# First layer and first head: probabilities turned by 32x32 blocks and transfers, and a program order held in a table

## Chip, cores and metric

The kernel runs on one core of one Trainium2 chip. The metric is the device time in microseconds (us) of one execution, given as the median of several; less is better. Five engines work side by side: TensorE (in the profile PE, its weight loads PEld), VectorE (DVE), ScalarE (ACT), GpSimd (POOL) and SyncE (SP), which here only issues transfers. Each takes its own instructions in program order, so an instruction that waits holds up everything behind it on its engine.

## What is computed

Two blocks in float32, over 2 sequences of 1024 tokens and 256 channels. The first is causal attention with one head of width 256, the second causal attention with 16 heads of width 128 and rotary positions, followed by a mixture of four experts. The reference, cut:

```python
x_norm = (x - mu) / sqrt(var + EPS) * gamma + beta          # first layer
q, k, v = x_norm @ qkv[:, :256], x_norm @ qkv[:, 256:512], x_norm @ qkv[:, 512:]
attn = softmax(where(causal, q @ k.T / sqrt(256), -inf))
x = layernorm(x + (attn @ v @ o_proj + x))
...
h = layernorm(x, ln1_w, ln1_b)                              # second layer
q, k, v = h @ wq + bq, h @ wk + bk, h @ wv + bv             # 16 heads of 128
q, k = rotary(q), rotary(k)
probs = softmax(where(causal, q @ k.T / sqrt(128), min))
h = x + (concat(probs @ v) @ wo + bo)
m = top2_of_4_experts(layernorm(h, ln2_w, ln2_b))
out = layernorm(x + (h + m))
```

## The kernel before

**Rows and steps.** Attention is cut into rows, one for each block of 128 queries. `RowA(b, i)` is row i (0 to 7) of sequence b in the first layer, `RowB(u, i)` the same of a unit u, that is one head of one sequence in the second layer. There are 16 RowA and 32 units of 8 RowB, in all 272 steps; step t starts the scores of row t. A0 = 16 is the step of the first RowB, and unit 0 is steps 16 to 23. `step(t, fillers)` writes out the instructions of a step: scores of row t, fillers registered for that step by `at`, `first`, `mid`, `end_of` and `late`, then the normalisation, transposition and output of rows that started one to ten steps earlier. The program order of all engines comes from this loop, and after the last step from a list written by hand (`all_of`, `hidden`, `m_bias`, `m_residual`, `o_stats`, `o_finish`: experts and the last normalisation).

**A row.** TensorE makes the scores in PSUM (L365, L780). `softmax_row` lets VectorE cut the diagonal block by a mask (L324) and take the maximum (L326), and ScalarE the exponential with its sum (L331). The probabilities then lie with queries on the partitions. The product with the values needs them the other way round, with keys on the partitions. There are two ways to turn them:

- `transposed_row` (L343): TensorE transposes each 128x128 block against the identity into PSUM; ScalarE copies the first four blocks of a row to SBUF (L348), VectorE the others (L346). All RowA, all of unit 0 and the first four rows of the last unit go this way. Of a RowA the turned tile `pTa` is the stationary operand of the product (L387), and the division by the row's sum comes with the residual (L395). In unit 0 VectorE divides first (L796).
- By blocks (units 1 to 31, apart from those four rows): ScalarE divides (L794), VectorE transposes each 32x32 block in place in the row (L811, `STREAM_TRANSPOSE`), and after four rows `gather` issues sixteen transfers on SP's queue (L833) that put the blocks where the whole transposition has them. The tile is then the moving operand of the product (L854), mostly eight to ten steps after the scores, as the table PARTS says. `blocks_sb` are two SBUF areas for the block form: `pair_sb`, and the tile `x1` of the first layer's output, which goes to DRAM first (`x1_out`) and comes back for the end (`x1_back`).

**Work beside the rows.** `b_project` and `seven_products` make queries, keys and values (seven products in place of eight, on sums that GpSimd and VectorE form); GpSimd turns queries and keys by their positions, four instructions for each half of a head (`rotated`, L477 to L479), which wait in a list and are written out at the end of a step. `a_residual` scales a tile of `x1` on ScalarE (L438), and GpSimd adds the output bias into the residual tile `h` (L441). `output_sums`/`seven_outputs` project a head pair onto `h`. Weights of later groups are loaded on SP's queue.

Of the kernel before, what the change touches and what calls it, by code (L numbers as in the profile page):

```python
# [18 lines left out]
P = 128  # L19
# [4 lines left out]
TABLE = "natural_log_exp_and_others"  # L24


@with_exitstack
def kernel(
# [62 lines left out]
    bank = [0]  # L91

    def acc_tile(k=None):

        bank[0] = 1 - bank[0] if k is None else k
        return ps_acc.tile([P, 512], F32, tag=f"acc{bank[0]}", name="pa")
# [25 lines left out]
    pair_sb = const.tile([P, 2 * 4 * D], F32, name="pair_sb")  # L122
    x1_dram = dpool.tile([P, NTT, D], F32, name="x1_dram")
    xr = x.rearrange("b (n p) d -> p (b n) d", p=P)
    a_ctx = ExitStack()
    apool = a_ctx.enter_context(tc.tile_pool(name="apool", bufs=1))
# [84 lines left out]
    def transposed(dst, xn, c, wcol, bcol):  # L211
# [13 lines left out]
    va = [apool.tile([P, NT, D], F32, tag=f"va{b}", name="va") for b in range(B)]  # L225
    wT = va[1].rearrange("p i d -> p (i d)")[:, : 3 * DC * D].rearrange(
        "p (w c n) -> p w c n", w=3, c=DC
    )
# [121 lines left out]
    pTa = work.tile([P, 2, NT, P], F32, tag="pT0", name="pTa", bufs=1)  # L350

    class RowA:


# [3 lines left out]
        def scores(self):  # L358
# [13 lines left out]
            self.pr, self.sm, _ = softmax_row(sc, i)  # L372

        def normalise(self):
            self.rs = small.tile([P, 1], F32, tag="rsa", name="rsa")
            nc.vector.reciprocal(self.rs, self.sm)

        def transpose(self):
            pT = pTa[:, self.i % 2]
            transposed_row(self.pr, self.i, lambda c0, n: pT[:, c0 : c0 + n, :])  # L380
            self.pT = pT

        def output(self):
            b, i = self.b, self.i
            pa = acc_tile()
            for c in range(i + 1):
                nc.tensor.matmul(  # L387
                    pa[:, :D],
                    lhsT=self.pT[:, c, :],
# [44 lines left out]
    def a_residual(b, i):  # L434
# [6 lines left out]
        nc.gpsimd.tensor_tensor(h[:, b * NT + i, :], t, bo_sb, ALU.add)  # L441
# [28 lines left out]
    def rotated(t, cs, eng=nc.gpsimd):  # L470

        def rest():
            rot = bpool.tile([P, 512], F32, tag="rot", name="rot")
# [51 lines left out]
    def weight_sums(name):  # L525
        t = lpool.tile([P, 3, HD], F32, tag=f"S{name}", name="S")
# [15 lines left out]
    def seven_products(g, b, name, wide):  # L542
# [35 lines left out]
        def kept(pa, i):  # L578
            t = lpool.tile([P, 512], F32, tag="part", name="part", bufs=2)
            moved(t, pa, i)  # L580
            return t
# [16 lines left out]
        def p1():  # L598
# [3 lines left out]
            st["k"] = bank[0]  # L602
# [28 lines left out]
        def p7():  # L631
# [3 lines left out]
            bank[0] = st["k"]  # L635

        if wide:
            return [p1, p2, p4, p3, p6, p5, p7]
        return [p1, p2, p3, p4, p5, p6, p7]
# [53 lines left out]
    def seven_outputs(g, b):  # L693
        st = {}

        def piece(bank_, w, x, start, i, k):
            def run():
                if start:
                    if bank_ == "a":
                        st["a"] = acc_tile()  # L700
                        st["k"] = bank[0]
# [18 lines left out]
                bank[0] = st["k"]  # L720

            return run
# [24 lines left out]
    blocks_sb = pair_sb, x1.rearrange("p n d -> p (n d)")  # L747
    NU = B * H
    U0, U1, GP = 1, (NU - 1, NU), 2
# [3 lines left out]
        1: {8: range(0, 2), 9: range(2, 4), 10: range(4, 8)},  # L753
        (NU - 2, 1): {8: range(0, 4), 9: range(4, 8)},
# [5 lines left out]
    class RowB:  # L760
# [12 lines left out]
        def scores(self):  # L773
# [13 lines left out]
            self.pr, self.sm, self.exponential = softmax_row(sc, i, self.blocks)  # L787
# [10 lines left out]
        def pT_tile(self, j):  # L798
            shape = [P, 4 * (j + 1), 512]
            if self.u == units[-1] and j == 0:  # L800
                return bpool.tile(shape, F32, tag="vg", name="pT")
            return work.tile(shape, F32, tag=f"pT{j}", name="pT", bufs=1)

        def transpose(self):
            i, j = self.i, self.i // 4
            if self.blocks:


                n = 4 * (i + 1)
                z = blocks_sb[j].rearrange("p (m i s) -> p i m s", i=4, s=32)  # L810
                nc.vector.transpose(  # L811
                    z[:, i % 4, :n, :], self.pr[:, : n * 32].rearrange("p (m s) -> p m s", s=32)
                )
# [8 lines left out]
        def gather(self, part):  # L822

            i, j = self.i, self.i // 4
            n = 4 * (j + 1)
            if part == 0:
                pTs[self.u, j] = self.pT_tile(j)
            pT = pTs[self.u, j]
            z = blocks_sb[j].rearrange("p (c b x) -> p b c x", b=4, x=P)
            for d in range(part * 4 // GP, (part + 1) * 4 // GP):  # L830
                for b in range(4):
                    a = (b + d) % 4
                    nc.sync.dma_start(pT[ts(b, 32), :, ts(a, P)], z[ts(a, 32), b, :n])  # L833

        def output(self, lag):
# [5 lines left out]
            if (g, b) not in aT:  # L841
                aT[g, b] = bpool.tile([P, GH, S], F32, tag="aT", name="aT")
# [32 lines left out]
    steps = [(RowA(b, i), []) for b in range(B) for i in range(NT)]  # L875
# [7 lines left out]
    steps += [(RowB(u, i), []) for u in units for i in range(NT)]  # L883

    firsts, mids, ends, lates = {}, {}, {}, {}

    def at(step, f, *args):
        steps[step][1].append(lambda: f(*args))

    def first(step, f, *args):  # L890
        firsts.setdefault(step, []).append(lambda: f(*args))

    def mid(step, f, *args):
        mids.setdefault(step, []).append(lambda: f(*args))

    def end_of(step, f, *args):
        ends.setdefault(step, []).append(lambda: f(*args))
# [9 lines left out]
    def late(step, f, *args):  # L907
        lates.setdefault(step, []).append(lambda: f(*args))


    XS0 = (14, 14, 15, A0 + 3)
    XS1 = (A0 + 8, A0 + 9, A0 + 10, A0 + 11)
# [5 lines left out]
    weights_transposed(0)  # L918
    a_stats(0, J0)
    weights_transposed(1)  # L920
    a_norm(0, 0)
    a_stats(0, J1)
    weights_transposed(2)
    weight_product(wqk, 0, lambda kc: wT[:, 1, kc, :], SCALE_A)
    parameters(0)
    for c in range(DC):
        a_transposed(0, 0, c)
    a_norm(0, 1)
    weight_product(wvo, 2, lambda kc: op_sb[:, kc, :], 1.0)
    a_query(0, 0, 0)  # L930
    a_query(0, 0, 1)
    a_transposed(0, 1, 0)
# [560 lines left out]
```

## Time and profile before

| | |
|---|---|
| median of 3 runs | 1172.46 us (1172.44 to 1173.12) |
| the profiled execution | 1174.3 us, of which the span from the first to the last instruction is 1172.5 us |
| mean granted TensorE clock | 0.996 |
| busy: TensorE | 1144.5 us (98%) |
| busy: VectorE | 846.2 us (72%) |
| busy: ScalarE | 641.5 us (55%) |
| busy: GpSimd | 808.3 us (69%) |

Busy time is a sum over the span; the stages differ. From 0 to about 110 us the first layer runs, from there to about 1040 us the heads, and after that the experts. A row of the groups' view reads: source line, engine, operation, output and inputs, shape, count, then busy time in us and mean ns of one, then idle time of the engine just ahead of it and who ended it. Matrix products in float32 appear as two instructions each, transpositions as one. Matmuls overlap, so the mean duration of one is longer than its distance to the next; the distance is what it costs in a full stream.

### The profile page before, as it was taken

The page shows a single profiled execution, that of the slowest core. Times are in us where ns is not written, and L with a number is a line of the kernel's source. Part 1 is how long each engine was busy: PE and PEld are TensorE (multiplying, and loading weights), DVE is VectorE, ACT ScalarE, POOL GpSimd, SP SyncE. Part 2 cuts the span into 40 slices and gives each one's busy share as a digit, 9 for nine tenths or more (in the row PEclk, how much of TensorE's full clock was granted, in tenths as well). Part 3 has the DMA queues.
Part 4 walks back from the last instruction along what each step waited for, and adds up shares of the span by engine and source line. Part 5 has one row for each costly group of instructions (what it writes and reads, how often), then busy time and mean ns, then how long its engine had stood idle before and what let it go on. Part 6 is the DMA issues. An engine that isn't in the chain of part 4 may idle for free.

```text
span 1172.5 us, 15932 instructions
## 1 busy us (share of the span) xinstructions
PE 1144.5 (98%) x4736; PEld 730.4 (62%) x4736; DVE 846.2 (72%) x1802; ACT 641.5 (55%) x1221; POOL 808.3 (69%) x758
## 2 busy tenths in 40 slices
PE   7999989999999999999999999999999999999997
PEld 5675745475756565666656565757575656656665
DVE  4555686778787868686868687877778788576575
ACT  3334256566566565656565656566656556452344
POOL 4005999988897989698969896989889998003100
PEclk9999999999999999999999999999999999999999
DMA  6000012566555555555555545555555668404011
GB/s 185 0 1 0 28 72 56 128 134 135 132 120 124 118 135 118 117 119 135 117 120 114 133 108 121 139 134 129 134 137 134 147 133 174 107 23 138 1 37 36
DMA packets 222965, 122.36 MB, mean 104 GB/s; under 512 B 17340, under 2 KB 221184, under 8 KB 222368
## 3 DMA queue, kind: packets, MB, share of 16 engines
q1 hardware_dynamic: 217696, 111.35, 40.7%
q0 software_dynamic: 1776, 4.89, 1.6%
q10 hardware_dynamic: 3408, 5.11, 1.2%
q8 instruction: 38, 0.62, 0.2%
q14 instruction: 47, 0.39, 0.1%
HBM read 20.62 MB, written 4.19 MB: 21 GB/s over the span
## 4 chain that ended last, share of the span: by engine, by line
PE 91%; DVE 5%; ACT 1%; DMA 1%; SPq 1%; issue 1%; ACTq 0%; DVEq 0%
PE av L854 20%; PE sc L780 20%; PE pa L562 11%; PE pa L553 5%; PE pa L708 5%; PE pa L1275 5%; PE pe L1298 4%; PE pc L562 4%; PE sc L365 3%; PE pa L387 2%; PE pc L553 2%; PE pc L708 2%; PE pa L660 1%; PE pa L306 1%; PE pa L293 1%; PE pt L343 1%
## 5 line engine op out<-in xcount | busy, mean ns | idle before, releaser
L794 ACT ACTIVATE pr<-pr,rs 128x640 f32<-128x640 f32 (+1 forms) x244 | 190.5, 781 | 219.2 <-DVE rs L792 219.0
L780 PE MATMUL sc<-Twk,Twq 128*128 128x512 f32 (+3 forms) x768 | 291.8, 489 | 2.0 <-ACT pr L331 1.9
L331 ACT ACTIVATE pr<-sc,nmx 128x128 f32<-128x128 f32 (+7 forms) x272 | 201.1, 739 | 150.0 <-DVE nmx L326 122.9
L854 PE MATMUL av<-pT,vg 128*128 128x512 f32 (+3 forms) x768 | 269.8, 489 | 2.3 <-DVE rs L792 1.2
L854 PEld LDWEIGHTS av<-pT,vg 128*128 128x128 f32 x768 | 144.1, 191 | 130.4 <-issue 101.3
L477 POOL TENSOR_TENSOR rot<-Twk,rope_sb 64x512 f32<-64x512 f32 x128 | 166.8, 1304 | 68.0 <-DVE Twk L595 61.1
L326 DVE TENSOR_REDUCE nmx<-sc 128x1 f32<-128x128 f32 (+7 forms) x272 | 206.2, 758 | 9.4
L780 PEld LDWEIGHTS sc<-Twk,Twq 128*128 128x128 f32 x768 | 136.2, 191 | 122.2 <-issue 107.0
L477 POOL TENSOR_TENSOR rot<-Twq,rope_sb 64x512 f32<-64x512 f32 x128 | 167.6, 1309 | 8.8
L324 DVE TENSOR_TENSOR sc<-sc,limit 128x128 f32<-128x128 f32 x272 | 79.7, 293 | 102.4 <-PE sc L780 82.0
L811 DVE STREAM_TRANSPOSE x<-pr 128x640 f32<-128x640 f32 (+1 forms) x124 | 128.5, 1036 | 12.4 <-ACT pr L794 10.8
L479 POOL TENSOR_TENSOR Twk<-Twk,rot 128x512 f32<-128x512 f32 x64 | 87.1, 1360 | 5.0
L478 POOL TENSOR_TENSOR Twk<-Twk,rope_sb 128x512 f32<-128x512 f32 x64 | 86.2, 1347 | 5.0
L478 POOL TENSOR_TENSOR Twq<-Twq,rope_sb 128x512 f32<-128x512 f32 x64 | 82.0, 1281 | 5.0
L479 POOL TENSOR_TENSOR Twq<-Twq,rot 128x512 f32<-128x512 f32 x64 | 81.4, 1273 | 5.0
L1167 POOL TENSOR_TENSOR hx<-hx,x 128x256 f32<-128x256 f32 x16 | 12.7, 826 | 93.0 <-DVE hx L1307 80.8
L441 POOL TENSOR_TENSOR hx<-x,bo_sb 128x256 f32<-128x256 f32 x16 | 12.2, 765 | 76.8 <-ACT x L438 76.8
L811 DVE STREAM_TRANSPOSE pair_sb<-pr 128x128 f32<-128x128 f32 (+1 forms) x120 | 60.1, 501 | 0.3 <-DMA we_sb<-in_L_ffn_we_dram 0.2
L1275 PE MATMUL pa<-xT,we_sb 128*128 128x512 f32 x128 | 57.5, 592 | 0.0
L870 ACT ACTIVATE aT<-av,par 128x512 f32<-128x512 f32 x64 | 43.7, 683 | 24.8 <-PE av L854 24.7
L717 DVE TENSOR_TENSOR hx<-hx,pa 128x512 f32<-128x512 f32 x70 | 46.5, 680 | 14.7 <-PE pa L708 14.7
L1298 PE MATMUL pe<-lent,hT 128*128 128x256 f32 x240 | 54.6, 380 | 0.0
(212 smaller groups left out, 1888.4 us busy)
## 6 DMA issues: line engine op xcount, KB each, us to landing
pT<-x SPq DMA_DIRECT2D x496, 128.0 KB, 2.7
pT<-pair_sb SPq DMA_DIRECT2D x480, 64.0 KB, 2.0
wk_g<-in_L_ffn_wk_dram SPq DMA_DIRECT2D x9, 256.0 KB, 3.0
wq_g<-in_L_ffn_wq_dram SPq DMA_DIRECT2D x9, 256.0 KB, 3.0
wv_g<-in_L_ffn_wv_dram SPq DMA_DIRECT2D x9, 256.0 KB, 3.0
wo_g<-in_L_ffn_wo_dram SPq DMA_DIRECT2D x9, 256.0 KB, 2.8
x_dram<-x ACTq DMA_DIRECT2D x2, 1024.0 KB, 3.9
x<-x_dram SPq DMA_DIRECT2D x2, 1024.0 KB, 6.4
```

The costliest lines, as they stand in the source:

```text
L326: nc.vector.tensor_reduce(nmx, sc[:, :L], AX.X, ALU.max, negate=True)
L331: nc.scalar.activation(pr[:, :L], sc[:, :L], AF.Exp, bias=nmx, accum_out=sm)
L477: nc.gpsimd.tensor_tensor(rot[lo, :], t[hi, cs], rope_sb[hi, 1, cs], ALU.mult)
L478: eng.tensor_tensor(t[:, cs], t[:, cs], rope_sb[:, 0, cs], ALU.mult)
L479: nc.gpsimd.tensor_tensor(t[:, cs], t[:, cs], rot, ALU.add)
L562: nc.tensor.matmul(pa, lhsT=w, rhs=x, start=start, stop=True, skip_group_check=True)
L780: nc.tensor.matmul(sc[:, ds(n0, n)], lhsT=qT[:, ts(i, P)], rhs=kT[:, ds(n0, n)], start=True, stop=True,)
L794: nc.scalar.activation(self.pr[:, :L], self.pr[:, :L], AF.Copy, scale=rs)
L811: nc.vector.transpose(z[:, i % 4, :n, :], self.pr[:, : n * 32].rearrange("p (m s) -> p m s", s=32))
L854: nc.tensor.matmul(cut(av), lhsT=vg[g, b][:, c, ts(hh, HD)], rhs=cut(pT[:, c, :]), start=(c == 0), stop=(c == i),)
L1275: nc.tensor.matmul(ph, lhsT=we1_sb[:, e, c, ts(m, P)], rhs=x2T[:, c, ds(k0 * P, 512)], start=(c == 0), stop=(c == DC - 1),)
L1298: nc.tensor.matmul(pe[:, ts(n, D)], lhsT=hTs[b, j, e][:, c, ts(k, P)], rhs=we2_sb[e][:, c, :], start=(c == 0), stop=(c == IC - 1),)
```

## The change

1. All RowA and unit 0 take the block way (`U0` from 1 to 0, `RowA.blocks = True`). They use areas of their own, `blocks_a`: a tile of the values' buffers, and `aT_sb`, a fixed place for what were rotating tiles of attention outputs. Both are cleared once by GpSimd. Since a RowA's probabilities are a stationary operand, `collect` copies the gathered blocks into a contiguous ring in `lent[b]`: ScalarE for the first four blocks of a row and for all of sequence 1, GpSimd for the others of sequence 0. A RowA's output comes 6 to 8 steps after its scores (`OUT_A`), where it came 3 after.
2. What follows a RowA moves with it: `a_rfinish`, `a_apply`, `x_transposed`, `a_residual`, the first projections (step 13 to 14) and the first sums (`XS0`, `XS1`).
3. `a_residual` no longer adds the bias. `h` is loaded from the DRAM copy of `x1` on SP's queue (`h_load`, 1 MB for each sequence), and GpSimd adds the bias in place (`h_bias`), late, from about step 28 on.
4. The seven products made during pair 0 use a bank of the transpositions as a third accumulator, as those of later pairs did. `acc_tile` keeps its hands off a bank that holds an unfinished sum.
5. At the start `weights_transposed(1)` and `product_qk` are ahead of the first statistics and of `weights_transposed(2)`.
6. The whole program is written down as named pieces (`do`), and a table MOVES of some 330 entries puts single pieces ahead of others, in the first layer and the first pairs and then from about step 240 to the end. Between those two stretches the order is that of the step loop.

```diff
+MOVES = (
+    ("o_finish 1 1 1", "o_stats 1 1 2"),
+    ("m_rstd 1 4", "m_rstd 1 5"),
+    ("all_of 1 1 1", "expert 1 1 2.0.3.0"),
...
+    ("m_rstd 1 4.5.6.7", "o_stats 0 0 0.1.2.3"),
...
+    ("hidden 0 0 0", "RowB.transpose 262"),
...
+    ("h_bias 1 0", "RowB.transpose 40"),
...
+    ("h_load 0", "RowB.scores 24"),
+    ("x1_out 1", "h_load 0"),
...
+    ("b_project 0.0.0 wk 0", "RowA.output 7"),
...
+    ("RowA.scores 6", "RowA.gather 3 1"),
...
+    ("a_transposed 0 1 0", "a_transposed 0 1 1"),
+)
+def ordered(ops, moves):
+    names = [key for key, _ in ops]
+    for key, before in moves:
+        names.remove(key)
+        names.insert(names.index(before), key)
+    by_name = dict(ops)
+    return [by_name[key] for key in names]
...
+    blocks_a = bpool.tile([P, 16 * P], F32, tag="vg", name="za"), aT_sb.rearrange(
+        "p k c s -> p (k c s)"
+    )
+    for z in blocks_a:
+        nc.gpsimd.memset(z, 0.0)
+    def blocks_of(z, pr, i):
+        n = 4 * (i + 1)
+        z = z.rearrange("p (m i s) -> p i m s", i=4, s=32)
+        nc.vector.transpose(
+            z[:, i % 4, :n, :], pr[:, : n * 32].rearrange("p (m s) -> p m s", s=32)
+        )
+    def gathered(pT, z, j, part):
+        n = 4 * (j + 1)
+        z = z.rearrange("p (c b x) -> p b c x", b=4, x=P)
+        for d in range(part * 4 // GP, (part + 1) * 4 // GP):
+            for b in range(4):
+                a = (b + d) % 4
+                nc.sync.dma_start(pT[ts(b, 32), :, ts(a, P)], z[ts(a, 32), b, :n])
...
         def transpose(self):
-            pT = pTa[:, self.i % 2]
-            transposed_row(self.pr, self.i, lambda c0, n: pT[:, c0 : c0 + n, :])
-            self.pT = pT
+            blocks_of(blocks_a[self.i // 4], self.pr, self.i)
...
+        def collect(self):
+            b, i = self.b, self.i
+            pT = pTa[b, i // 4].rearrange("p c (a i s) -> p c i a s", a=4, i=4)
...
+                if c0 < 4 or b:
+                    nc.scalar.copy(shaped, src)
+                else:
+                    nc.gpsimd.tensor_copy(shaped, src)
...
-        nc.gpsimd.tensor_tensor(h[:, b * NT + i, :], t, bo_sb, ALU.add)
+    def h_load(b):
+        nc.sync.dma_start(h[:, ts(b, NT), :], x1_dram[:, ts(b, NT), :])
+    def h_bias(b, i):
+        t = h[:, b * NT + i, :]
+        nc.gpsimd.tensor_tensor(t, t, bo_sb, ALU.add)
...
-    U0, U1, GP = 1, (NU - 1, NU), 2
+    U0, U1 = 0, (NU - 1, NU)
...
+        (0, 0): {10: range(0, 4)},
...
+    OUT_A = dict(zip(range(2 * NT), (8, 8, 9, 9, 12, 12, 13, 13, 16, 16, 17, 17, 20, 20, 21, 21)))
...
-            keys = seven_products(ng, nb, "wk", wide)
-            queries = seven_products(ng, nb, "wq", wide)
+            keys = seven_products(ng, nb, "wk", wide or not k)
+            queries = seven_products(ng, nb, "wq", wide or not k)
...
+    do(weights_transposed, 0)
+    do(weights_transposed, 1)
+    do(a_stats, 0, J0)
+    do(product_qk)
+    do(parameters, 0)
+    do(a_norm, 0, 0)
+    do(weights_transposed, 2)
...
+    for f in ordered(ops, MOVES):
+        f()
```

## Prediction

> **What bounds the kernel now.** I read the page first, then the groups of TensorE by form, the busy time by stretches, and the timelines of the places where a stretch is not full.
>
> ```profile
> PE 1144.5 (98%) x4736; PEld 730.4 (62%) x4736; DVE 846.2 (72%) x1802; ACT 641.5 (55%) x1221; POOL 808.3 (69%) x758
> ...
> PE   7999989999999999999999999999999999999997
> ```
>
> TensorE bounds: 28.0 us idle in a span of 1172.5. Time can go in two ways, by taking instructions off TensorE or by filling its 28 us.
>
> ```profile
> L343 PE MATMUL pt<-ident,pr 128*128 128x128 f32 x118 | 17.8, 274 | 4.6 <-DVE pr L796 4.0 <-DVE xT L218 0.6
> ```
>
> These 118 are the transpositions of `transposed_row`: 36 for the eight rows of a sequence (1+2+...+8), so 72 in the first layer, 36 in unit 0, 10 in the last unit. They overlap, so 274 ns isn't their price. The timeline of TensorE gives that:
>
> ```profile
> 133.59 1.04 PE L343 MATMUL pt<-ident,pr 128*128 128x128 f32 x8
> 134.46 3.19 PE L387 MATMUL pa<-va,pTa 128*128 128x256 f32 x14
> ...
> 151.51 0.55 PE L343 MATMUL pt<-ident,pr 128*128 128x128 f32 x3 [3.17 <-DVE pr L796]
> 151.87 2.75 PE L780 MATMUL sc<-Twk,Twq 128*128 128x512 f32 x4
> ```
>
> Eight take 134.46 - 133.59 = 0.87 us: 0.109 each. The last two lines show a TensorE that waited 3.17 us for unit 0's division on VectorE.
>
> ```profile
> 0.00:20.00 20.00, 12.89 (x43) 8.90 (x44) 7.91 (x27) 6.28 (x12) 11.65 (x30) 1.00 0.90 243
> 20.00:110.00 90.00, 90.00 (x380) 62.36 (x379) 49.16 (x133) 33.51 (x76) 12.65 (x12) 1.00 0.02 7
> ...
> 150.00:160.00 10.00, 8.49 (x26) 4.73 (x27) 8.54 (x16) 4.87 (x10) 9.30 (x14) 0.83 0.26 107
> ...
> 200.00:960.00 760.00, 758.98 (x3179) 472.18 (x3178) 583.16 (x1144) 456.72 (x873) 654.85 (x596) 1.00 0.55 127
> 960.00:1085.00 125.00, 121.72 (x519) 81.33 (x518) 89.07 (x215) 63.16 (x108) 41.77 (x41) 0.99 0.48 113
> ```
>
> (TensorE, weight loads, VectorE, ScalarE, GpSimd.) The idle time is at the ends: 7.1 us before 20 us, 9.0 from 110 to 200, 1.0 from 200 to 960, 3.3 up to 1085, 0.8 at 1096, 6.8 behind the last product. From 150 to 160 VectorE (85%) and GpSimd (93%) are nearly full too.
>
> **The change, part by part.**
>
> *Transpositions leave TensorE*: 72 + 36 = 108 x 0.109 = **-11.7 us**, all on the path, since TensorE is full around nearly all of them.
>
> *What replaces them.* For eight rows VectorE does eight block transpositions, by the rows of L811 by form (two shown) 0.30, 0.43, 0.57, 0.70, 0.84, 0.97, 1.10, 1.24 = 6.15 us.
>
> ```profile
> L811 DVE STREAM_TRANSPOSE x<-pr 128x1024 f32<-128x1024 f32 x31 | 38.4, 1238 | 8.7 <-ACT pr L794 8.7
> ...
> L811 DVE STREAM_TRANSPOSE pair_sb<-pr 128x128 f32<-128x128 f32 x30 | 9.0, 299 | 0.3 <-DMA we_sb<-in_L_ffn_we_dram 0.2
> ```
>
> In the first layer they replace 1.94 us of copies (L346): +8.4 for two sequences. In unit 0 they replace the same copies and a division of 6.4 us (L796) that goes to ScalarE at 6.2 (L794) against 4.0 of copies (L348): VectorE -2.2, ScalarE +2.2. `collect` has ScalarE copy what L348 copied, plus 1.9 for sequence 1; GpSimd gets four copies of 128 to 512 columns. Their nearest row, a GpSimd 128x512 operation at 1.49, bounds them at 0 to 6 us; I take 4, in a stretch where GpSimd is nearly idle (12.65 of 90 us). Two clearings of 128x2048, at 0.22 for 128 columns, are 0.2 to 3.5 us each, behind transfers needed much later: nothing.
>
> Is VectorE still beside TensorE? Steps 0 to 7: TensorE scores 15.5, queries, values and their transpositions 14.6, together 30 us; VectorE minima 2.3, maxima 6.1, reciprocals 1.2, block transpositions 6.15, statistics and norms 8, evacuations 2: 26. Steps 8 to 15: TensorE 45, VectorE 36. Steps 16 to 23 (unit 0 with the outputs of sequence 1): TensorE outputs 15.5, scores 7.8, projections and values 17, first pieces 3: 43; VectorE softmax 16, outputs with statistics 9, norms 8, evacuations 4, sums 4: 41. So it holds, tightly in the last stage.
>
> *The rule against it.* The Trainium skill, "VectorE: DVE Perf Modes", section "Rules for kernel authors", advises TensorE for a 128x128 transposition that may land in PSUM; VectorE only turns 32x32 blocks. In this trace VectorE's 18.4 us for the 108 blocks is indeed longer than TensorE's 11.7: counted by engine time, the rule makes the change a loss of 6.7. But TensorE is 98% busy and VectorE 72%, so I count by the bounding engine.
>
> *Transfers.* Six groups of sixteen more on SP's queue, 0.62 us each to issue (L833, in the view of pT: shortest, median and longest issue in ns) and 2.4 to land: 12.4 us a group.
>
> ```profile
> L833 SPq DMA_DIRECT2D pT<-x x496: 585/616/1795, 201.0 to 1063.0; - x166
> ```
>
> A group of RowA has three steps of cover (rows 0 to 3: step 5 to step 8), 15 to 18 us of TensorE's work. So nothing, with 3 us to spare at the first. `h_load` (2 x 1 MB, 6.4 us each by x's way back) goes through the same queue, behind `x1_out` (3.9); gathers behind it have some five steps of slack. If all that cover were gone, each group would cost its lateness.
>
> *GpSimd.* From 102.2 to 256 us it never pauses over 1.2 us, and it feeds the heads: the sixteen rotations (5.35 us each) of the first two head pairs' tiles, sums (7), and 12 of `a_residual`'s additions (0.77 each). The scores at 205.7 use a tile finished at 203.0, 2.7 us earlier. The change takes the additions out of this stretch (-9) and puts 12.2 us back from step 28 to 55. The first projection, now at 96.0, comes earlier by the start (3.3), 42 transpositions (4.5) and outputs of 11 blocks not yet issued (11 x 0.43 = 4.7): at about 84, the first rotation some 4 later. The chain of 15 rotations and sums, 87 us, would be through at 175, TensorE wants it at about 181. Later the slack of 9 us at step 48 (tile done 238.8, needed 248) goes: GpSimd gains about 24 minus up to 12, TensorE comes 23 earlier; up to 2 us of waiting.
>
> *Start.* The timeline of TensorE again:
>
> ```profile
> 8.43 1.09 PE L245 MATMUL pt<-ident,lent 128*128 128x128 f32 x4 [2.35 <-DMA lent<-in_L_attn_qkv_dram]
> 10.15 3.78 PE L256 MATMUL pa<-va 128*128 128x256 f32 x8 [0.63 <-ACT va L250]
> ...
> 14.38 1.54 PE L215 MATMUL pt<-ident,pair_sb 128*128 128x128 f32 x8 [0.26 <-DVE par L234]
> ```
>
> The third weight tile lands at 8.4 us and holds up the first product, which needs only the first two; ScalarE's copy of the second (9.53) sits behind the statistics. Reordered, the product starts at about 6.8 instead of 10.15. The first transpositions of x then wait for the norm (done 11.0) and not for the product: 11.1 instead of 14.38, **-3.3 us** (bounds 0, if the statistics are displaced, to -3.6).
>
> *Waits from 110 to 200.* 9.0 us: 4.0 for unit 0's division, which no longer stands ahead of TensorE; 1.2 for its reciprocal; the rest for a full VectorE and ScalarE. With six to ten steps between a row and its product, and the table's moves, I take 5.0 of the 9.0 away and leave 4.0 for VectorE (41 of 43 us) and GpSimd. Bounds: 9 away, or 4 added. Behind the gaps the products are also slower: L780's four took 2.55 instead of 1.72, the next 2.15. By the trace about **-1.0** goes with the gaps. "TensorE: Matmul & The Clock Gate", section "Part 1: The HAM clock gate", has the clock halved after some 3.4 us of idleness, for as long: an estimate of 1.7.
>
> *End.* The moves among rows 243 to 271 bring transpositions and experts forward into 3.3 us of idle time; I take -1.5 (0 to -3.3, and +1 if VectorE or ScalarE is made late). `m_rstd 1 4.5.6.7` ahead of other statistics frees the second norm: -0.8 (0 to -0.8). The last chain (four additions, statistics, root, scale, transfer) keeps its order for the last tile: 0.
>
> Sum: 11.7 + 3.3 + 5.0 + 1.0 + 1.5 + 0.8 = 23.3 us. From the profiled execution's own 1174.3 that is 1151.0; its time is 1.8 above the median of the runs, so the median should be **1149**.
>
> **Rivals.**
> *GpSimd or VectorE takes over in the heads' first stages*: the -5.0 and -1.0 don't come, or 2 us of GpSimd at step 48 are added. For: GpSimd 93 to 96%, VectorE 85% at 150 us. Against: additions moved away, 12 us of earlier start. 1149 + 6 + 2 = 1157.
> *Everything fills*: all 9.0, 3.3 and 0.8 go: 1149 - 4 - 1.8 = 1143, a little less if gaps elsewhere go.
> *Slower: SP's queue takes over.* The gathers stand in order on one queue; if each transfer costs 1.9 us to issue (the longest of L833) and 6.4 to land, a group takes 37 us against 16 of cover. Four groups in the first layer, each 21 late, lose 84: 1233. It decides from 23.3 / 4 = 5.8 us of lateness, that is 22 us a group. Against: the median is 0.62, and then the queue is otherwise empty (DMA share 0.02 from 20 to 110 us).
> *The order table does nothing*: transpositions and start alone, 1172.5 - 15 = 1157.5, in the range of the first rival.
>
> **Numbers.** Main case 60% (1144 to 1154), first rival and idle table 27% (1154 to 1162), all filled 8% (1139 to 1144), slower 3%, about as before 2%. A measurement here can tell 0.2%, 2.3 us. Range 1141 to 1160. Faster 0.95, same 0.02, slower 0.03.
>
> **What would show it.** L343 at x10; TensorE's busy time near 1133; L811 at x268 (244 now), taking 18 us more; the first product near 6.8 us; first rotation before 92; TensorE idle under 6 us from 110 to 200 of the old program, with unit 1's rows 20 us earlier. Wrong if TensorE waits for pTa or lent (gathers, `collect`) by more than 2 us in the first layer, or for rotated tiles behind step 32, or if the span falls by less than 14.

## The result and the profile after

The changed kernel takes 1167.72 us (median of 7 runs, 1163.02 to 1168.37), the kernel before 1172.46 us on the same chip. The ratio is 0.9952 with a 95% interval of 0.9938 to 0.9966. That is a gain of 4.7 us; the prediction said 23.3 us (1149) with a range of 1141 to 1160. Faster was right; the size and the range were wrong.

The page of the changed kernel, its engine row and its TensorE slices. The profiled execution's own time is the median, 1167.72 us:

```profile
span 1165.9 us, 15853 instructions
...
PE 1132.4 (97%) x4628; PEld 720.1 (62%) x4628; DVE 856.8 (73%) x1806; ACT 645.2 (55%) x1227; POOL 812.5 (70%) x762
...
PE   6999979999999999999999999999999999899997
```

TensorE has 108 instructions less and is busy 12.1 us less (1144.5 before). But the span fell by only 6.6 us, because TensorE's idle time rose from 28.0 to 33.5 us. The first slice, 7 before, is now a 6. The busy time by stretches (columns: TensorE, weight loads, VectorE, ScalarE, GpSimd, granted clock, DMA share, GB/s) says where:

```profile
0.00:20.00 20.00, 9.26 (x31) 6.52 (x32) 9.85 (x15) 4.92 (x8) 16.48 (x32) 0.85 0.82 232
20.00:110.00 90.00, 89.98 (x345) 60.40 (x344) 58.92 (x152) 35.67 (x83) 13.15 (x12) 1.00 0.23 56
...
140.00:200.00 60.00, 52.58 (x196) 30.02 (x196) 42.78 (x85) 38.62 (x76) 56.57 (x56) 1.00 0.59 144
200.00:240.00 40.00, 37.73 (x133) 21.84 (x133) 31.92 (x58) 20.54 (x38) 38.25 (x34) 0.96 0.61 127
...
960.00:1085.00 125.00, 120.45 (x500) 80.79 (x499) 85.42 (x220) 59.98 (x101) 34.04 (x34) 0.97 0.43 104
```

Stretch less busy time gives TensorE's idle time. The same sum for the kernel before, for what the prediction left idle, and for two of the experiments below:

| TensorE, us | before | predicted | after | clearing on VectorE | and two sums earlier |
|---|---|---|---|---|---|
| idle, 0 to 20 | 7.1 | 3.8 | 10.7 | 5.3 | 5.2 |
| idle, 20 to 110 | 0.0 | 0.0 | 0.0 | 0.0 | 0.0 |
| idle, 110 to 240 | 9.6 | 4.6 | 9.7 | 10.6 | 6.7 |
| idle, 240 to 960 | 0.4 | 0.4 | 1.5 | 1.9 | 3.8 |
| idle, 960 to 1085 | 3.3 | 1.8 | 4.6 | 4.4 | 1.8 |
| idle behind 1085 | 7.6 | 6.8 | 7.0 | 6.7 | 7.0 |
| busy in all | 1144.5 | 1131.8 | 1132.4 | 1130.6 | 1130.4 |

(The prediction's waits were stated from 110 to 200; the 0.6 us that the kernel before idles from 200 to 240 is left in its column; its busy time is 1144.5 less 11.7 and 1.0.) So the transpositions went about as reckoned. Four terms did not come: the start, which got worse, the waits of the middle, the clock behind the gaps (the mean granted clock is 0.991, 0.996 before), and the end. The start is the largest single miss, and its timeline shows it (start, duration, engine, line, operation; in brackets the idle time ahead of it and its releaser). First the norm of the kernel before, then the change:

```profile
9.65 1.38 DVE L209 TENSOR_SCALAR pair_sb<-x,mvx,rsx 128x256 f32<-128x256 f32 x4 [0.60 <-ACT rsx L206]
```

```profile
7.04 3.76 PE L610 MATMUL pa<-we_flat 128*128 128x256 f32 x8 [0.67 <-ACT we_flat L604]
...
11.07 7.29 DVE L560 TENSOR_SCALAR pair_sb<-x,mvx,rsx 128x256 f32<-128x256 f32 x4
...
11.53 0.33 PE L566 MATMUL pt<-ident,pair_sb 128*128 128x128 f32 x1
...
12.28 1.85 POOL L710 MEMSET za<- 128x2048 f32 x1
14.02 3.55 POOL L710 MEMSET aT_sb<- 128x4096 f32 x1
...
17.77 1.97 PE L566 MATMUL pt<-ident,pair_sb 128*128 128x128 f32 x7 [5.92 <-DVE pair_sb L560]
```

The first product starts at 7.04 us (10.15 before) and the first transposition of x at 11.53 (14.38 before), as planned. Then TensorE waits 5.92 us for VectorE's norm of four tiles. That norm takes 7.29 us here, and took 1.38 us before. It is four instructions of 0.41 us; the first went through, the second lasted 6.33 us. GpSimd's two clearings run from 12.28 to 17.57, and 0.2 us later TensorE gets its next tile. In the 10 us from 10 to 20 the granted clock is 0.70.

The waits of TensorE, for the rest (engine, line, what it waited for, us in all, times, longest):

```profile
PE pt L566 <- DVE pair_sb L560: 7.7, 3, 5.9
PE av L1272 <- DMA pT<-pair_sb: 6.2, 2, 4.2
...
PE sc L1206 <- ACT pr L685: 2.7, 4, 1.4
PE pc L982 <- POOL S L949: 1.9, 1, 1.9
PE sc L1206 <- POOL Twq L899: 1.5, 1, 1.5
```

Behind the start there is not one large wait but several small kinds: exponentials, two more norms of VectorE (1.8 of the first row's 7.7), a sum and a rotated tile of GpSimd's, and two gathers, one of 2.0 us ahead of 235 and one of 4.2 us at 995, in the last rows.

### The profile page after: what moved, and what is told of

Read it like the earlier page. It is cut to its first block, busy times and chain, and to the rows that moved or that the text cites. A ratio compares the mean times of both kernels' runs of the same rounds, so it can differ in the third digit from the quotient of the medians.

```text
span 1165.9 us, 15853 instructions
## 1 busy us (share of the span) xinstructions
PE 1132.4 (97%) x4628; PEld 720.1 (62%) x4628; DVE 856.8 (73%) x1806; ACT 645.2 (55%) x1227; POOL 812.5 (70%) x762
## 4 chain that ended last, share of the span: by engine, by line
PE 86%; POOL 5%; DVE 3%; DMA 2%; SPq 2%; ACT 1%; issue 1%; ACTq 0%; POOLq 0%; DVEq 0%
PE av L1272 20%; PE sc L1206 18%; PE pa L982 10%; PE pa L973 6%; PE pa L1130 5%; PE pa L1746 5%; PE pe L1769 4%; PE pc L982 4%; PE sc L751 3%; PE pc L973 2%; POOL rot L897 2%; PE pc L1130 2%; SPq L732 2%; PE pa L800 1%; PE pa L647 1%; PE pa L660 1%
## 5 line engine op out<-in xcount | busy, mean ns | idle before, releaser
L1223 ACT ACTIVATE pr<-pr,rs 128x128 f32<-128x128 f32 (+5 forms) x252 | 195.7, 780 | 226.8 <-DVE rs L1221 226.8
L685 ACT ACTIVATE pr<-sc,nmx 128x256 f32<-128x256 f32 (+7 forms) x272 | 200.7, 738 | 119.8 <-DVE nmx L680 90.4
L897 POOL TENSOR_TENSOR rot<-Twq,rope_sb 64x512 f32<-64x512 f32 x128 | 167.1, 1305 | 10.4 <-ACT Twq L925 1.7
L1746 PE MATMUL pa<-xT,we_flat 128*128 128x512 f32 x128 | 57.8, 597 | 0.0
L1288 ACT ACTIVATE aT_sb<-av,par 128x512 f32<-128x512 f32 x64 | 43.7, 683 | 19.2 <-PE av L1272 15.0
L685 ACT ACTIVATION_READ_ACCUMULATOR pr<-sc,nmx 128x1 f32 x272 | 53.5, 197 | 0.0
```

The lines of the kernel that those rows point to most:

```text
L685: nc.scalar.activation(pr[:, :L], sc[:, :L], AF.Exp, bias=nmx, accum_out=sm)
L897: nc.gpsimd.tensor_tensor(rot[lo, :], t[hi, cs], rope_sb[hi, 1, cs], ALU.mult)
L1223: nc.scalar.activation(self.pr[:, :L], self.pr[:, :L], AF.Copy, scale=rs)
L1746: nc.tensor.matmul(ph, lhsT=we1_sb[:, e, c, ts(m, P)], rhs=x2T[:, c, ds(k0 * P, 512)], start=(c == 0), stop=(c == DC - 1),)
```

## The experiments

The theories after the result. A: the clearings hold VectorE's norm, and all of that comes through to the end. B: the clearings matter little or are absorbed, since a later wait takes their place. For the middle: the order in which GpSimd, or SP's queue, does its pieces; or the work of an engine; or something else.

**1. Clearing on VectorE.** VectorE has nothing to do before the first tile of x lands (4.96 us in the change), so it can clear the areas itself.

```diff
-        nc.gpsimd.memset(z, 0.0)
+        nc.vector.memset(z, 0.0)
```

> The changed kernel with the two clearings of the block areas on VectorE in place of GpSimd, where VectorE waits for the first tile of x. Theory A (GpSimd's clearings, 1.85 + 3.55 us, hold up VectorE's first norm, which took 7.29 us instead of 1.38, and TensorE's 5.9 us wait behind it is lost for good, because all later chains start from there): the first norm takes 1.4 us again, TensorE's wait of 5.9 us falls under 1 us, and the time falls by 5 to 7 us, to about 1161 to 1163. Theory B (the first layer has slack, and GpSimd's rotations or VectorE set the time up to 200 us whatever the start does): the wait goes, but the idle time from 140 to 200 us grows by about as much, and the time stays within 2 us of 1167.7.

1160.79 us (1156.22 to 1161.47), ratio to the kernel before 0.9884 (0.9864 to 0.9904): by the medians 6.9 us less than the change as made, by the two ratios 8.0. Its timeline:

```profile
1.26 1.76 DVE L710 MEMSET za<- 128x2048 f32 x1 [0.40 <-issue]
...
3.83 3.47 DVE L710 MEMSET aT_sb<- 128x4096 f32 x1 [0.80 <-issue]
...
6.88 3.78 PE L610 MATMUL pa<-we_flat 128*128 128x256 f32 x8 [0.68 <-ACT we_flat L604]
...
10.96 1.38 DVE L560 TENSOR_SCALAR pair_sb<-x,mvx,rsx 128x256 f32<-128x256 f32 x4
...
11.43 1.74 PE L566 MATMUL pt<-ident,pair_sb 128*128 128x128 f32 x8
```

The statistics begin later (7.21 us in place of 4.96), but the norm begins when it did. It takes 1.38 us again, and the transpositions run as one group of eight. The wait of 5.9 us is gone and nothing comes in its place. Theory A: the clearings cost about 6.9 us. In the profiled spans it is 6.5: TensorE is idle 4.7 us less, and busy 1.8 us less at a mean granted clock of 0.996 in place of 0.991. GpSimd, without the clearings, also issues the loads of weights earlier (12.63 us, 17.47 in the change), but that is not where the time comes from: TensorE's idle time from 110 to 240 us is not less (10.6 against 9.7).

**2. The same clearings in the kernel before**, on GpSimd and at the same place, into tiles not used at that time.

```diff
+    nc.gpsimd.memset(hx[:, 2048:4096], 0.0)
+    nc.gpsimd.memset(xT.rearrange("p c s -> p (c s)"), 0.0)
```

> The kernel before, with two clearings of the same sizes (2048 and 4096 columns) added to GpSimd at the same place, into areas that are written later anyway. Nothing else changes. Theory A: VectorE's first or second norm is held up by up to 5.5 us, TensorE waits as long, and the time rises by 3 to 6 us over 1172.5. Theory B: the first layer's TensorE is full and later waits absorb it: less than 1.5 us. Rival C (the norm was held by something else in the changed kernel, for instance the transfers of weights or its own new order): no norm is longer than 1.5 us, and the time is unchanged.

1172.68 us (12 runs), ratio 1.0 (0.9991 to 1.0009): nothing. This miss says which instruction is held. Its timeline:

```profile
9.53 1.38 DVE L209 TENSOR_SCALAR pair_sb<-x,mvx,rsx 128x256 f32<-128x256 f32 x4 [0.60 <-ACT rsx L206]
...
11.90 0.40 DVE L200 BATCH_NORM_STATS2 st<-x 128x6 f32<-128x256 f32 x1
12.06 1.85 POOL L351 MEMSET hx<- 128x2048 f32 x1
...
12.43 0.40 DVE L200 BATCH_NORM_STATS2 st<-x 128x6 f32<-128x256 f32 x1
...
13.81 3.56 POOL L352 MEMSET xT<- 128x4096 f32 x1
...
15.38 0.81 DVE L218 TENSOR_SCALAR hx<-pt,par 128x512 f32<-128x512 f32 x1 [1.19 <-PE pt L215]
16.11 2.37 DVE L209 TENSOR_SCALAR pair_sb<-x,mvx,rsx 128x256 f32<-128x256 f32 x4
```

The first norm is over before the clearings begin. The statistics beside the first clearing take 0.40 us, as without it, and the copy out of PSUM beside the second takes 0.81, which is its time elsewhere too. Only the second norm, SBUF to SBUF as the first, is held: 2.37 us in place of 1.38, while the clearing runs to 17.37. TensorE has other products then. So theory A's 3 to 6 us did not come, and its rival C, that no norm is held, falls too. The clearings cost something only where this one kind of instruction meets them on the path.

**3. Clearing on GpSimd in twelve pieces.** If VectorE could get in between two instructions of GpSimd, it would lose one piece's time at most.

```diff
-        nc.gpsimd.memset(z, 0.0)
+        for k in range(z.shape[1] // 512):
+            nc.gpsimd.memset(z[:, ts(k, 512)], 0.0)
```

> The changed kernel with GpSimd's two clearings cut into twelve of 512 columns, at the same place in its order. Theory A (an instruction of VectorE that reads and writes SBUF by itself waits for the whole clearing that runs): each of the four parts of the first norm waits for one piece of about 0.45 us at most, the norm takes 2 to 3.5 us in place of 7.29, and the time is 1161.5 to 1164. Rival B (GpSimd shuts VectorE out as long as any of its clearings is left): still near 7 us, time within 2 us of 1167.7.

1167.47 us (13 runs), ratio 0.9938 (0.9917 to 0.9959), as the change was. The profiled run:

```profile
11.33 7.48 DVE L560 TENSOR_SCALAR pair_sb<-x,mvx,rsx 128x256 f32<-128x256 f32 x4
...
11.84 0.92 PE L566 MATMUL pt<-ident,pair_sb 128*128 128x128 f32 x3
...
12.99 1.94 POOL L711 MEMSET za<- 128x512 f32 x4
14.85 3.81 POOL L711 MEMSET aT_sb<- 128x512 f32 x8
...
18.86 1.33 PE L566 MATMUL pt<-ident,pair_sb 128*128 128x128 f32 x5 [6.11 <-DVE pair_sb L560]
```

Three of the norm's four instructions were through before the first piece. The fourth was not let in between any two pieces: it lasted until the last one ended at 18.66, 6.52 us in place of 0.41, as the duration of these four shows (shortest, median, longest in ns):

```profile
L560 DVE TENSOR_SCALAR pair_sb<-x,mvx,rsx x4: 406/406/6517, 11.3 to 12.3; 128x256 f32<-128x256 f32 x4
```

TensorE waited 6.11 us, up to 18.86. So theory A (one piece at most) is out and rival B holds in this run. It is also a close race: the fourth instruction was due to end 0.3 us before the first piece begins. Four of the 13 runs took 1158 to 1161 us and the other nine 1166 to 1170. The four may be runs in which the whole norm was through ahead of the clearings, or in which it did get in between; no profile shows one of them.

**4. The order table, cut in two.** Both kernels have the clearings on VectorE. The first keeps only the entries from step 240 on (90 of 332), the second only those before (242). The first lines that each leaves out:

```diff
-    ("wv.0.1 p4", "wv.0.1 p3"),
-    ("load_weights 2 wq", "rotation 29"),
...
```

```diff
-    ("o_finish 1 1 1", "o_stats 1 1 2"),
-    ("m_rstd 1 4", "m_rstd 1 5"),
...
```

> The changed kernel with the clearings on VectorE (as in e1, 1160.8 us), and of the order table only the entries for step 240 to the end: the first layer and the first pairs in the order of the step loop. Theory A (the block way lengthens the wait from a row to its product, and the table's moves are what keeps TensorE full from 20 to 140 us, while 9.8 us of waits from 140 to 240 are left by GpSimd's chain, VectorE and the transfers): without them more than 8 us of idle time appear before 140 us, in all 1170 to 1185. Rival B (the moves at this end do nothing, as in the prediction's third rival): within 2 us of 1160.8.

> As e1, and of the order table only the entries up to step 68: from step 240 to the end the order is that of the loop and the list, as in the kernel before. Theory A (the moves at the end fill the old idle times at 996 to 1035 and 1096 us, but bring a product ahead of its transfer, 4.4 us at 989, so that nothing is gained on the whole): idle time behind 960 us of 10 to 12 us as before, time within 2 us of 1160.8. Rival B (they gain what was predicted, 2.3 us, and something else was lost): 1163. Rival C (they lose): 1158.

Without the start's entries: 1186.87 us, ratio 1.0124 (1.0107 to 1.0141), which is 26.1 us slower than with them and slower than the kernel before. TensorE's waits in that kernel:

```profile
PE pa L558 <- ACT lent L547: 7.5, 4, 4.4
PE sc L964 <- POOL Twq L657: 5.1, 2, 3.3
PE pc L731 <- POOL S L707: 5.0, 1, 5.0
```

The first is the product of a RowA waiting for `collect`, the very wait that the block form adds. TensorE is idle 10.4 us from 20 to 140, where the change as made is full. Without the end's entries: 1160.67 us, ratio 0.9896 (0.9882 to 0.9911), the same as with them. So the start's part of the table carries the change, and the end's part gives nothing that these intervals show.

**5. The start's new order alone**, in the kernel before: first product ahead of the statistics, third weight tile behind.

```diff
-    a_stats(0, J0)
...
-    a_norm(0, 0)
-    a_stats(0, J1)
-    weights_transposed(2)
...
+    a_stats(0, J0)
...
+    a_norm(0, 0)
+    weights_transposed(2)
...
+    a_stats(0, J1)
```

> The kernel before with only the start in the new order (the first two weight tiles and their product ahead of the statistics' consumers and of the third tile). Theory A (TensorE is full from 20 to 110 us, so a start 3.3 us earlier comes through): first product near 6.9 us, first layer 3 us earlier, time 1169 to 1170.5. Rival B (the later waits for VectorE, from 110 to 200 us, take it back): 1171.5 to 1172.5.

1170.33 us, ratio 0.9985 (0.9972 to 0.9999): by the ratio 1.7 us (0.1 to 3.3); by the medians, with 1173.4 for the kernel before on that chip, 3.1. The medians contain the clock: five of its eight runs had a mean granted clock of 0.998 or 0.999, of the kernel before five of 20. The first transposition of x came 2.5 us earlier (11.86) but the transpositions near 20 us only 1.6 us (19.31 in place of 20.92).

**6. GpSimd's order in the middle.** With the clearings on VectorE, two entries are put behind the table's last.

```diff
+    ("scale_queries #2", "weight_sums wq"),
+    ("output_weight_sums", "rotation 14"),
```

> As e1, with two pieces of GpSimd put later: the scaling of the second group's queries behind the sums of its keys, and the sums of the output weights behind the rotations 12 and 13. Theory A (GpSimd's chain ends last from 105 to 177 us): TensorE's waits for S (1.9 us at 141) and for Twq (1.5 us at 177) go, and the time falls by 2 to 4 us to 1157 to 1159. Rival B (VectorE and ScalarE are as late there): those two waits go, others grow by as much, time within 1 us of 1160.8.

1157.47 us (1156.38 to 1159.77), ratio 0.9871 (0.9857 to 0.9886). By the medians that is 3.3 us less than experiment 1, by the ratios, whose intervals overlap, 1.5; no version that computes everything has a lower median. In the profiled spans it is 4.5 us, nearly all of it idle time of TensorE (4.3). Its waits from 110 to 245 us:

```profile
PE av L1274 <- DMA pT<-pair_sb: 2.8, 1, 2.8
PE pt L568 <- DVE pair_sb L562: 1.9, 2, 1.0
PE sc L1208 <- POOL Twq L901: 1.0, 1, 1.0
PE sc L1208 <- ACT pr L687: 0.8, 2, 0.5
PE pc L984 <- POOL S L951: 0.2, 1, 0.2
```

The wait for GpSimd's sum `S` fell from 1.9 to 0.2 us, that for the rotated tile from 1.5 to 1.0, and with them those for the exponential from 2.2 to 0.8. Some is given back: a wait of 1.9 us for another `S` stands at 350 us, and 240 to 960 is idle for 3.8 us. The idle time at the end fell by 2.6 us, from the same two entries 800 us earlier.

**7. One of a rotation's four instructions on VectorE**, for pair 1's queries (on the change as made).

```diff
-    HELP = ()
+    HELP = ("wq",)
```

> The changed kernel with one of the four instructions of each rotation of the second pair's queries (four rotations) on VectorE in place of GpSimd: 4 x 1.28 us less on GpSimd between 177 and 200 us, 4 x about 0.9 more on VectorE. Theory A (GpSimd's chain of rotations from 93 to 183 us is what ends last there): TensorE's wait of 1.5 us for Twq at 183 goes, the time falls by 1 to 3 us. Rival B (VectorE, 85 to 97% busy from 110 to 170 us, is as late): no gain, or 1 us lost, with the waits named VectorE's.

1182.73 us, ratio 1.0076 (1.006 to 1.0093), 15 us slower than the change. Rival B had the direction, but this does not test GpSimd's load alone, for VectorE's own waits name another reason:

```profile
DVE Twq L898 <- POOL rot L897: 14.3, 4, 7.3
```

VectorE takes its instructions in order, and it now waits 14.3 us for GpSimd's half of the rotation, with the rows' maxima and norms queued behind it.

**8. Less work for GpSimd, for VectorE, for both.** Three kernels on top of experiment 6: the last addition left out of the first 16 rotations; the maximum of the first three units' rows over every second column; and that addition left out together with maxima over the diagonal block alone. The first and the third leave a part of the computation out, so they only say what the time would be. The diagonal maxima by themselves gave no time: with them some exponentials are not finite, so not every maximum will do, and the second kernel takes every second column.

```diff
-            nc.gpsimd.tensor_tensor(t[:, cs], t[:, cs], rot, ALU.add)
+            if n >= 16:
+                nc.gpsimd.tensor_tensor(t[:, cs], t[:, cs], rot, ALU.add)
```

```diff
-        nc.vector.tensor_reduce(nmx, sc[:, :L], AX.X, ALU.max, negate=True)
+        nc.vector.tensor_reduce(nmx, sc[:, 0:L:every], AX.X, ALU.max, negate=True)
...
+        nc.vector.tensor_reduce(nmx, sc[:, first:L], AX.X, ALU.max, negate=True)
```

> As f1 (1157.5 us), with the last of the four GpSimd instructions left out of the first 16 rotations (pairs 0 and 1): the rotated part isn't added to queries and keys there. GpSimd has about 21 us less to do between 88 and 200 us. Theory A (GpSimd's chain sets the time from 105 to 200 us even after f1): the idle time from 140 to 240 us falls from 6.4 to under 3.5 us, time 1153 to 1155. Rival B (after f1 VectorE, ScalarE and the transfers set it): idle time and time unchanged within 1 us.

> f1_sums, with the maximum of the rows of the first three units taken over every second column (any value that keeps the exponential in range gives the same softmax): with half of each maximum's time saved some 0.4 us less of VectorE for each of 24 rows, about 9 us from 110 to 240. Theory V (VectorE's row work makes the remaining waits of 6.4 us there): idle falls to about 4 us or less, time about 1155. Theory O (the order of rows and transfers makes them): idle stays at 5.5 to 7 us, time 1157 to 1158.

> The same short maxima together with the first 16 rotations without their last addition (left out of the computation). Theory V: with both engines relieved nothing is left to wait for but transfers: idle from 110 to 240 about 1 to 3 us, time 1151 to 1153. Theory O: idle stays at 5 to 7 us, time 1154.5 to 1156.

| | GpSimd | VectorE | both |
|---|---|---|---|
| time, us | 1155.17 | 1160.90 | 1153.22 |
| ratio to before (95%) | 0.9846 (0.9825 to 0.9866) | 0.99 (0.9872 to 0.9929) | 0.9838 (0.9821 to 0.9854) |
| idle 110 to 240, us | 6.6 | 6.6 | 5.3 |
| TensorE busy in all, us | 1130.3 | 1131.3 | 1128.1 |

Experiment 6 had 6.7 us idle there and 1130.4 busy. In the row of 140 to 200 the lightened engine is seen, and TensorE (first figure) hardly moves; first the kernel with less for GpSimd (fifth figure; 56.88 in experiment 6):

```profile
140.00:200.00 60.00, 54.91 (x198) 30.27 (x197) 47.11 (x93) 40.42 (x77) 50.46 (x48) 1.00 0.58 141
```

then the one with less for VectorE (third figure; 45.86 in experiment 6):

```profile
140.00:200.00 60.00, 56.23 (x195) 30.78 (x194) 41.84 (x91) 40.08 (x77) 56.79 (x57) 0.97 0.57 139
```

and with both lightened:

```profile
140.00:200.00 60.00, 55.90 (x200) 30.82 (x199) 40.86 (x93) 41.82 (x80) 51.52 (x49) 1.00 0.56 142
```

Without GpSimd's additions the waits for it go, but those for the exponential rise from 0.8 to 3.1 us. The amount of work of neither engine makes most of this idle time; with both relieved 5.3 us remain. But the time with both relieved fell by 4.2 us all the same, more than theory O allowed. In the profiled spans it is 2.9 us, and 2.3 of them are TensorE's busy time: the granted clock (the sixth figure) is 1.00 from 140 to 200, where experiment 6 has 0.97. So how the idle time is divided counts too, and not only its sum. The kernel with half maxima is by the medians 3.4 us slower than experiment 6 (the intervals overlap); its profile has a wait for a gather of 4.5 us at 989, in rows that it doesn't touch.

**9. The transfers.** The second `h_load` moves 1 MB on SP's queue at 217 us, just ahead of a gather. In the change as made the SP timeline is

```profile
206.18 10.91 SPq L732 DMA_DIRECT2D pT<-pair_sb  x16
217.13 0.59 SPq L856 DMA_DIRECT2D hx<-x_dram  x1
217.83 12.70 SPq L732 DMA_DIRECT2D pT<-x  x16
```

The sixteen transfers of the gather behind the load land 5.9 us after their issue at the median and 6.8 at most, where 2.7 is the median of all; the gather that follows on the queue (`pT<-pair_sb`) is the one for which TensorE waits 2.0 us, up to 234.94. Three kernels move the load: to ScalarE's queue; to step 24, with the product of row 255 put behind the first expert's hidden layer; and, from experiment 6, ahead of an earlier gather, that of rows 28 to 31.

```diff
-            nc.sync.dma_start(h[:, ts(b, NT), :], x1_dram[:, ts(b, NT), :])
+            nc.scalar.dma_start(h[:, ts(b, NT), :], x1_dram[:, ts(b, NT), :])
```

> The changed kernel with the two loads of h (1 MB each) issued on ScalarE's queue in place of SP's. Theory A (the second load, issued at 217.1 us among the gathers, makes a gather of x land in 6.8 us instead of 2.7 because the transfers share the engines, so TensorE waits 2.0 us at 233): the queue alone doesn't matter, the wait remains within 1 us, time within 1 us. Rival B (it is the order in SP's queue that delays the gathers): the wait of 2.0 us at 233 goes, time 1 to 3 us less.

1166.54 us, ratio 0.9925 (0.9894 to 0.9955). The time says nothing of the load: four of its eleven runs took 1157 to 1159 us and seven 1165 to 1173, and the profile, of the second group, has the wait at the start again:

```profile
11.84 0.71 PE L566 MATMUL pt<-ident,pair_sb 128*128 128x128 f32 x3
18.25 1.33 PE L566 MATMUL pt<-ident,pair_sb 128*128 128x128 f32 x5 [5.70 <-DVE pair_sb L560]
```

As in experiment 3, three parts of the norm were through and the fourth was held (6.12 us), so the faster four may be runs in which all four were through; that is not shown. Of the load the profile does say something: the gather `pT<-x` lands in 2.4 us at the median again, but `pT<-pair_sb` takes 3.6, and TensorE waits 2.2 us for it. This points to the order on the queue for the one; taking the load off the queue did not take TensorE's wait away.

```diff
+    ("h_load 1", "RowB.scores 24"),
+    ("RowB.output 255 8", "m_transposed 0 1 1"),
```

> As e1, with the second load of h directly behind the first (about 145 us instead of 211), and the product of row 255 behind the first expert's hidden layer in program order. Theory A (transfers end last at two places: a gather next to a load of 1 MB lands in 6.8 us instead of 2.7, TensorE waits 2.9 us at 229; and the moved product waits 4.4 us at 989 with other work behind it): both waits fall under 1 us, time 5 to 7 us less, 1154 to 1156. Rival B (the rows' pace on VectorE sets both places): the waits move to the next piece, less than 2 us gained.

1164.61 us, ratio 0.9926 (0.9911 to 0.9941): 3.8 us slower than experiment 1, which it changes in two places at once. The wait behind the load (2.9 us in experiment 1) is gone, but the product put later at the end uncovers a longer one:

```profile
994.94 3.78 PE L1748 MATMUL pa<-xT,we_flat 128*128 128x512 f32 x4 [6.13 <-DVE hx L1094]
```

```diff
+    ("h_load 1", "RowB.gather 31 0"),
```

> Clearings on VectorE (e1), the two pieces of GpSimd later (f1, 1157.5 us), and the second load of h ahead of the gather of rows 28 to 31, at about 178 us instead of 211. Theory A (the load next to the gather of row 39 is what TensorE waits for at 226, 2.8 us): that wait falls under 1 us, nothing else moves, 1154.5 to 1156. Rival B (row 39's own pace or the gather of row 31 is as late): within 1 us of 1157.5.

On top of experiment 6: 1159.97 us, ratio 0.9883 (0.9866 to 0.9901), no gain over it. From 200 to 240 the idle time falls from 2.8 to 0.6 us, and from 960 to 1085 it rises from 1.8 to 4.1, with a wait of 4.1 us for a gather. Taken one at a time, these waits move and don't vanish.

## Why the prediction was wrong

**Transpositions, -11.7: right, and rather too small.** TensorE's busy time fell by 12.1 us, and by 13.9 in experiment 1, whose mean clock is the 0.996 of the kernel before: 0.129 us for each of the 108, where the one place that the prediction measured gave 0.109. VectorE's block transpositions took no time from TensorE: the first layer stays full from 20 to 140 us. The Trainium skill's rule that a 128x128 transposition belongs on TensorE ("VectorE: DVE Perf Modes", in the prediction) was rightly set aside, for the bounding engine decides. But TensorE stays full only through the table (experiment 4); the prediction took that for granted.

**"Two clearings of 128x2048 ... are 0.2 to 3.5 us each, behind transfers needed much later: nothing": this step failed.** It looked for what is queued behind the clearings on GpSimd and found nothing urgent. It did not ask what runs beside them. It had the size of one wrong too (4096 columns, not 2048), but that was not the fault: 1.85 and 3.55 us are about what it allowed. They cost about 6.9 us (experiment 1) and turned the start's -3.3 into a loss: 10.7 us idle before 20 us where 3.8 were expected. The Trainium skill, "SBUF — State Buffer", section "Who interferes with whom", has the rule: VectorE and GpSimd share a pair of SBUF ports, a `tensor_scalar` from SBUF to SBUF can take the pair, and whoever is first keeps it for its whole instruction. The runs agree: of three kinds of VectorE instruction that met the clearings in experiment 2, only this one was held. The rule would let VectorE in after one instruction of GpSimd; in experiment 3's profile one VectorE instruction waited for twelve in a row (6.52 us), and the measurement decides. By the recorded starts VectorE was even first (the held instruction at 11.39 us, the first clearing at 12.28) and should have kept the pair; it was held all the same, and why stays open. That the clearings hold the norm is shown by experiment 1; that the ports are the reason rests on the rule and on which kinds were held.

**Start, -3.3: rather too large even without the clearings.** Its order alone gave some 1.7 us (experiment 5, interval 0.1 to 3.3). The first transposition did come earlier by 2.5 us; of that 1.6 were left near 20 us.

**Waits from 110 to 200, -5.0, and the clock behind the gaps, -1.0: failed.** Unit 0's division is gone from the waits, as foreseen, but as much came back as other waits: 9.7 us from 110 to 240 against 9.6. The clock went down with the new gaps instead of up (0.70 from 10 to 20 us, 0.96 from 200 to 240). Part of the waits is order: two of GpSimd's pieces stood in the wrong place, and moving them took 3.9 us of idle time from there (experiment 6). The prediction's GpSimd chain was near in length (90 us, 87 expected) and late in time: its first rotation starts at 93.25 us, not at 88, and ends its wanted tile at 183.37, not at 175. With the clearings on VectorE it starts at 86.6 and is through at 176.8, as reckoned; but TensorE wants the tile at 175.3 then, and waits 1.5 us as before. Both shift together, because GpSimd pauses 7.6 us at 98 for the second projections, which come from TensorE through ScalarE. The 6.7 us left by experiment 6 are for the most part not the amount of GpSimd's or VectorE's work (experiment 8). What makes them, the order of rows on ScalarE and SP or something else, stays open.

**End, -1.5 and -0.8: failed, 0 in place of 2.3** (experiment 4). The moves put the product of row 255 ahead of other work, and it waits 4.2 us at 995 for its gather; put behind the hidden layer, that layer waits 6.1 us for VectorE (experiment 9).

**Rivals.** "GpSimd or VectorE takes over" (1157) had the middle's number about right, for the 6 us did not come, but not its reason: lighter work on both engines left most of the waits. "The order table does nothing" (1157.5) was far off: without its start the kernel takes 1186.9. SP's queue is no bound in the first layer: a group of sixteen took 10.2 to 10.5 us to issue, and landed in 2.1 and 3.1 us at the median. Behind 1 MB it is late (experiment 9). No rival held what happened: a new instruction on an idle engine that stops a second engine on the path.

**The sum with what the runs showed.** 11.7 less of transpositions, 1.7 of the start and 6.9 back for the clearings make 6.5, and the middle and the end add nothing; measured were 4.7 (6.6 by the spans). Of the 18.6 us that are missing to 23.3, the clearings are 6.9, the middle with its clock 6.0, the end 2.3 and the start's size 1.6; 1.8 are left over. So the clearings are the largest single term, but without them the change would still have fallen short, by 10 to 12 us (experiment 1).

## What to carry to other kernels

Before an instruction on an idle engine is priced at nothing, look at what runs beside it and not only behind it: a clearing belongs where the engine that it may block has nothing urgent to do yet, here VectorE's first seven microseconds. When a full stream has many small waits with different releasers, price their sum as staying unless one order removes them together; here two relieved engines and three places for one transfer left most of it standing, there or elsewhere. An order table is to be valued part by part, with each part taken out once.

## What the runs showed of the hardware

- A SBUF-to-SBUF `tensor_scalar` on VectorE (four of 128x256, 1.38 us) took 7.29 us beside GpSimd's clearings of 128x2048 and 128x4096 (1.85 and 3.55 us); statistics (0.40 us) and a PSUM source (0.81 us) were not slowed. In each of four profiles with the clearings at that place (the change, experiments 3 and 7, the first of 9) a single one of the norm's four instructions was held, for 5.9 to 6.5 us in place of 0.41: the second, the fourth, the first, the fourth.
- Cutting the clearings in twelve pieces of 128x512 did not let VectorE in between them in the profiled run (one instruction of 6.52 us). VectorE clears as fast as GpSimd: 1.76 and 3.47 us.
- The transfers of a gather behind a 1 MB load on one queue landed in 5.9 us at the median (6.8 at most) in place of 2.7, and in 2.4 with the load on another queue (one profile of each).
- The wait of 5.92 us stands in a stretch (10 to 20 us) with a granted clock of 0.70. The next eight products of 128x256 took 2.56 us, and 1.89 us without the wait (experiment 1).
